# One fused two-layer kernel: sums moved to VectorE in the first layer, seven products for the last 96 columns, and another order of the last block, the start and the flag's load

## The chip, the core and the metric

The kernel runs on one core of one Trainium2 chip. The metric is device time in microseconds (us) of one launch. All times below are such times, taken from several runs or from one profiled execution; which of the two is said each time. A core has TensorE (PE, with its weight loads shown apart as PEld), VectorE (DVE), ScalarE (ACT), GpSimd (POOL) and SyncE (SP), which here issues all DMAs.

## The reference

`x` has 4 x 512 rows of 512 numbers; there are two gated layers with 1376 hidden columns each. Everything is 32-bit floating point.

```python
def attn(x, w_gate, w_up, w_down):
    s = silu(x @ w_gate.T)
    k = int(0.5 * 1376)
    _, idx = top_k(-abs(s), k)        # the half of smallest size in each row
    s = s with those set to 0
    return (s * (x @ w_up.T)) @ w_down.T

def ffn(x, W_gate, W_up, W_down):
    return (silu(x @ W_gate.T) * (x @ W_up.T)) @ W_down.T

x = x + layernorm(attn(layernorm(x), ...))
x = x + layernorm(ffn(layernorm(x), ...))
```

## The kernel before, in words

The 2048 rows are 16 tiles of 128. **First layer**: eight `Unit`s of two tiles. Each tile is loaded, normed (`layernorm`, L112), transposed by TensorE and copied to `xT` (`normed_T`, L339). `products` (L381) makes the gate as plain matmuls (L404, six groups a unit) and the up projection as a 2 x 2 block product with seven instead of eight block products (class `Seven`, L132: p1, p6, p5, then p7, p2, then p4, p3, each of 2 chunks). Its left factors are sums of quarters of `xT`: `Unit.sums` calls `stationary_sums` (L116) with GpSimd, four operations on 128 x 256 into the tile `S`. A 32-bit matmul is two instructions on TensorE. `search` (L435) finds each row's median size in six steps, in which ScalarE counts (L456) and VectorE takes the next guess (L461 to L481); `turns` (L554) transposes the masked hidden values, 128 at a time, and ScalarE copies them out (L582, L584).

**Down projections** of both layers are `downs` (L233): seven products too, for one or two pairs of tiles, as steps p1, p5, p6 for each pair, then p7, p2, p4, p3 for all pairs. Each step loads its weight (640 KB, tag `wd`, three buffers, L230) when it is first used. `rest` in it (L263) adds the last 96 hidden columns. `out_norm` (L321) norms the output tile (`moments`, L98: statistics, aggregate, add on VectorE, a power on GpSimd), adds the residual `xr` on GpSimd (L331) or, for the final tile, on VectorE (L328), and stores it (L332).

**Second layer**: four `Block`s of four tiles. `Block.pair` (L652) makes two chunks of 128 hidden columns of gate and up by seven products each, five times; `down_sums` (L690) makes their sums `D` on GpSimd. `Block.rest` (L674) makes the last 96 hidden columns of gate (`fg`) and up (`fu`) with plain matmuls of 512 columns (L681). Then the next block's tiles are normed and this block's `finish` (L706) runs its two pairs together; the last block runs them one after the other, `finish([0])` and `finish([1])`.

Whether the quick search found the exact median is counted in `flags`. The flag `badi` (L851) is loaded by all engines at the end (`values_load`, L875), and a general version of the layers is run behind a branch (L876) if it isn't zero, which it is here.

**What sets the order**: Everything in `tc.block(schedule_with_timeline_sim=True)` (L873) is put in order by a planner when the program is built. It simulates the engines and gives each engine, when it is free, the ready instruction that comes first in the program's order. So an instruction's place in the program is its rank, and a stall in the simulation is filled by a later ready instruction. On the chip each engine keeps that order and waits on semaphores. `fill` in `products` (L394) writes out by hand where other units' steps rank between the groups of matmuls. At the start the program ranks the load of tile 0, its norm, the load of tile 1, then the first layer's gate weight in three pieces (`CH`, L61) and the rest (L743 to L751). 18 transposes of the identity (L85) run before tile 0 is ready.

PSUM has tags `pa`, `px`, `py`, `pt` with two buffers each; in SBUF tags `S`, `w` (`sg` and the search's copy) have one.

Of the kernel before, what the change touches and what calls it, by code (L numbers as in the profile page):

```python
# [31 lines left out]
def sandwich_kernel(  # L32
# [65 lines left out]
    def moments(src, nm, kind, n=1):  # L98

        bufs = 1 if kind == "f" else 5  # L100
        st = small.tile([P, n, 6], F32, tag="st" + kind, name=f"st_{nm}", bufs=bufs)
        for i in range(n):
            nc.vector.bn_stats(st[:, i, :], src[:, ts(i, H // n)])
# [8 lines left out]
    def layernorm(dst, src, nm, kind):  # L112
        mv, rs = moments(src, nm, kind)
        nc.vector.tensor_scalar(dst, src, mv[:, 0:1], rs, ALU.subtract, ALU.mult)
# [17 lines left out]
    class Seven:  # L132


        def __init__(self, nm, left, right, c12, c21, c22):
            self.left, self.right = left, right
            self.c12, self.c21, self.c22 = c12, c21, c22
            n = c12.shape[-1]
            self.pa, self.px, self.py = [bank(k, f"{k}{nm}")[:, :n] for k in ("pa", "px", "py")]
# [93 lines left out]
    def downs(work, pairs, key, w_d, wr, res, dst, nm, final=False):  # L233
# [4 lines left out]

        st = []
# [11 lines left out]
        def product(k, which, i=None):  # L251
# [4 lines left out]
            for p in [st[i]] if first else st:  # L256
# [25 lines left out]
        def p7():  # L282
            product("p7", PX)
            for p in st:
                pz.append(bank("pt", f"pz{nm}_{p[0][0]}")[:, :H2])
                rest(pz[-1], p, 1, hi, True)

        def p2():
            product("p2", PA)
            for p, z in zip(st, pz):  # L290
                tiles, left, last, pa, px, py, ya, yb = p
                rest(pa, p, 0, lo)
                nc.vector.tensor_add(yb[:, hi], yb[:, lo], px)  # L293
                nc.vector.tensor_add(yb[:, hi], yb[:, hi], py)
                nc.vector.tensor_add(yb[:, hi], yb[:, hi], z)
                nc.scalar.copy(ya[:, lo], pa)

        def p4():
            product("p4", PX)
            for p in st:  # L300
# [5 lines left out]
        def p3():  # L306
            product("p3", PY)
            for p in st:
# [3 lines left out]
                out_norm(work, tiles[0], ya, res, dst, nm, final)  # L312
# [6 lines left out]
        return heads + [p7, p2, p4, p3]  # L319

    def out_norm(work, t, y, res, dst, nm, final=False):  # L321
# [3 lines left out]
        if final:  # L325
            mv, rs = moments(y, f"o{nm}_{t}", "f", 2)
            nc.vector.tensor_scalar(y, y, mv[:, 0:1], None, ALU.subtract)
# [20 lines left out]
    class Unit:  # L348
# [25 lines left out]
        def sums(self):  # L374
# [3 lines left out]
                nc.gpsimd, a[:, :2], a[:, 2:], b[:, :2], b[:, 2:], s[:, 0], s[:, 1], s[:, 2]  # L378
# [175 lines left out]
        def turns(self, other=False):  # L554
# [4 lines left out]
            def turn(k, g0):  # L559
# [22 lines left out]
                nc.scalar.copy(hT[:, g0 : g0 + nf, :], pt[:, :nf, :])  # L582
                if nf < n:
                    nc.scalar.copy(end, pt[: isz[-1], nf, :])  # L584
# [39 lines left out]
    class Block:  # L624
# [49 lines left out]
        def rest(self, wg, wu):  # L674
# [239 lines left out]
```

## Time and profile before

| | us |
|---|---|
| Median of 3 runs (886.12 to 889.33) | 888.31 |
| The profiled execution's own time | 887.46 |
| Its span, first to last instruction | 885.5 |
| TensorE busy | 862.3 |
| VectorE busy | 511.8 |
| ScalarE busy | 300.9 |
| GpSimd busy | 180.3 |

Mean granted TensorE clock: 0.993 of full speed. The profile gives each group of instructions its source line, engine, operation, output and inputs by the program's names, and shapes. A row of waits says which engine and instruction stood idle, for whom (the one that came last), for how long in total, how often, and the longest. Ends of matmuls are modelled, so their bars overlap; the distance between starts is the pace. A "q" behind an engine's name means its instruction queue. Times in the timeline count from the span's start. The first layer takes about the first 450 us, the second the rest.

### The profile page before, as it was taken

The numbers are of one execution on the slowest core, as the hardware profiler recorded it, in microseconds if no ns is written. First come the engines' busy times: TensorE is split into PE (matmuls) and PEld (weight loads), VectorE is DVE, ScalarE is ACT, GpSimd is POOL, SyncE is SP. The second block draws the span as 40 slices with busy tenths as digits, with TensorE's granted clock in tenths as the row PEclk, the third lists the DMA queues.
The fourth block names the chain that finished last, engine by engine and source line by source line (L and its number), as shares of the span: only waits on it lengthen the run. The fifth ranks groups of instructions, "written<-read, shape, count | busy, mean of one in ns | idle before, by whom it ended". The sixth has DMA issues, their size and how long they took to land. (4 is left out here: it accounts for less than half of the span.)

```text
span 885.5 us, 10211 instructions
## 1 busy us (share of the span) xinstructions
PE 862.3 (97%) x3588; PEld 652.4 (74%) x3588; DVE 511.8 (58%) x1328; ACT 300.9 (34%) x598; POOL 180.3 (20%) x249
## 2 busy tenths in 40 slices
PE   8999999999999899999999999999999999999995
PEld 5656566757667576677788888888788888888784
DVE  4887776775939578766955434554236443444322
ACT  2465575748463757466011111011101112011100
POOL 2120111212212112110433211321203221122221
PEclk9999999999999999999999999999999999999998
DMA  9999413334232343377374003610045002420064
GB/s 317 360 335 345 165 54 119 120 101 143 78 119 98 103 138 102 119 293 262 132 254 150 0 1 113 195 44 0 30 143 167 1 0 65 143 97 1 30 217 156
DMA packets 62924, 117.54 MB, mean 133 GB/s; under 512 B 4816, under 2 KB 36560, under 8 KB 62864
## 3 DMA queue, kind: packets, MB, share of 16 engines
q1 hardware_dynamic: 62864, 116.80, 39.4%
q8 instruction: 30, 0.49, 0.2%
q14 instruction: 30, 0.25, 0.1%
HBM read 97.91 MB, written 18.87 MB: 132 GB/s over the span
## 5 line engine op out<-in xcount | busy, mean ns | idle before, releaser
L456 ACT ACTIVATE ja<-v,cur 128x1376 bf16<-128x1376 f32 x96 | 138.3, 1441 | 76.9 <-DVE cur L481 54.4
L404 PE MATMUL pg<-wg,xT 128*128 128x456 f32 (+1 forms) x384 | 158.0, 559 | 3.4 <-ACT p L408 2.5
L404 PEld LDWEIGHTS pg<-wg,xT 128*128 128x128 f32 x384 | 73.2, 193 | 68.6 <-issue 59.9
L118 POOL TENSOR_TENSOR D<-hTb 128x256 f32<-128x256 f32 x20 | 14.6, 730 | 180.5 <-DVE hTb L672 180.5
L461 DVE TENSOR_SCALAR low<-cur 128x2 int32<-128x2 f32 x48 | 8.7, 181 | 72.0 <-ACT ja L456 72.0
L143 PE MATMUL pau<-wu,xT 128*128 128x344 f32 x128 | 43.6, 452 | 0.0
L143 PE MATMUL pagb<-xTb,wg 128*128 128x256 f32 x160 | 41.4, 379 | 0.0
L143 PE MATMUL paub<-xTb,wu 128*128 128x256 f32 x160 | 41.3, 380 | 0.0
L143 PE MATMUL pxub<-T,wu 128*128 128x256 f32 x160 | 41.2, 380 | 0.0
L143 PE MATMUL pxgb<-T,wg 128*128 128x256 f32 x160 | 41.1, 379 | 0.0
L258 PE MATMUL pad<-wd_p,hT 128*128 128x256 f32 x160 | 39.4, 380 | 1.3 <-DMA wd_p<-in_L_attn_w_down_dram 1.3
L408 ACT ACTIVATE p<-pg 128x456 f32<-128x456 f32 (+1 forms) x48 | 26.0, 544 | 43.1 <-PE pg L404 39.5
L258 PE MATMUL pxdb<-wdb_p,hTb 128*128 128x256 f32 x160 | 36.7, 379 | 2.1 <-DMA wdb_p<-sum_f 2.1
L258 PE MATMUL pxd<-wd_p,hT 128*128 128x256 f32 x160 | 37.2, 380 | 1.5 <-DVE y L293 1.5
L258 PE MATMUL padb<-wdb_p,hTb 128*128 128x256 f32 x160 | 37.1, 379 | 0.9 <-DMA wdb_p<-in_L_ffn_W_down_dram 0.9
L258 PE MATMUL pydb<-wdb_p,D 128*128 128x256 f32 x160 | 37.9, 379 | 0.1
L258 PEld LDWEIGHTS pxd<-wd_p,hT 128*128 128x128 f32 x160 | 30.3, 190 | 7.4 <-DVE y L293 1.7
L258 PEld LDWEIGHTS padb<-wdb_p,hTb 128*128 128x128 f32 x160 | 30.3, 190 | 7.2 <-issue 3.3
L258 PEld LDWEIGHTS pxdb<-wdb_p,hTb 128*128 128x128 f32 x160 | 30.3, 190 | 6.7 <-issue 2.5
L258 PEld LDWEIGHTS pad<-wd_p,hT 128*128 128x128 f32 x160 | 29.6, 190 | 7.4 <-DMA wd_p<-in_L_attn_w_down_dram 1.7
L258 PEld LDWEIGHTS pydb<-wdb_p,D 128*128 128x128 f32 x160 | 30.1, 190 | 6.2 <-issue 2.5
L670 ACT ACTIVATE sg<-sg 128x768 f32<-128x768 f32 x20 | 16.9, 843 | 50.9 <-DVE sg L167 50.9
(221 smaller groups left out, 1721.9 us busy)
## 6 DMA issues: line engine op xcount, KB each, us to landing
wd_p<-sum_a SPq DMA_DIRECT2D x28, 640.0 KB, 4.0
wd_p<-in_L_attn_w_down_dram SPq DMA_DIRECT2D x21, 640.0 KB, 4.2
wdb_p<-sum_f SPq DMA_DIRECT2D x20, 640.0 KB, 4.1
wdb_p<-in_L_ffn_W_down_dram SPq DMA_DIRECT2D x15, 640.0 KB, 4.2
xn<-in_x_dram SPq DMA_DIRECT2D x16, 256.0 KB, 3.1
xr<-in_x_dram SPq DMA_DIRECT2D x16, 256.0 KB, 2.8
x<-y SPq DMA_DIRECT2D x16, 256.0 KB, 2.0
xnb<-x SPq DMA_DIRECT2D x16, 256.0 KB, 3.1
```

The lines of the kernel that those rows point to most:

```text
L118: eng.tensor_add(s1, a21, a22)
L143: nc.tensor.matmul(ps, self.left[k][:, c, :], self.right[k][:, c, :], start=first and c == 0, stop=c == 1, skip_group_check=not first,)
L258: nc.tensor.matmul(p[which], p[1](k, c), ws[k][:, c, :], start=first and c == 0, stop=c == HC - 1, skip_group_check=not first,)
L404: nc.tensor.matmul(pg, self.xT[:, i, c, :], wg[:, c, c0:c1], start=(c == 0), stop=(c == NH - 1),)
L408: nc.scalar.activation(p[:, c0:c1], pg, AF.Silu)
L456: nc.scalar.activation(junk, v, AF.Sign, bias=cur[:, 0, i : i + 1], accum_out=cur[:, 1, i : i + 1],)
L461: nc.vector.tensor_scalar(low, cur[:, 1, :], 0.0, None, ALU.is_gt)
L670: nc.scalar.activation(sg[:, 1:, :], sg[:, 1:, :], AF.Silu)
```

## The change

1. `Unit.sums`: the four sums are made by VectorE instead of GpSimd.
2. `turns(True)` (only the last unit but one): the second tile's copies go from ScalarE to VectorE.
3. `downs`: the addition of `px` to `yb` moves from step p2 to p7; the remaining two additions become a step `c22`, called at the end of p2, or in the last block alone. In the last block both pairs run together, in the order p7, c22, p3, then p4 and p2 for the first pair and for the second. The last output's first half is read straight from PSUM by the statistics and the subtraction.
4. `Block.rest`: the last 96 columns of gate and up are one 2 x 2 block product (gate and up above each other, tiles left and right) by `Seven`. The sums of its weights are made once, by VectorE.
5. At the start the first piece of the gate weight is loaded before tile 1, and six transposes of the normed tile 0 into the unused `warm` are added.
6. `values_load` and the branch move into the planned stretch.

```diff
-    def moments(src, nm, kind, n=1):
+    def moments(parts, nm, kind):
+        n = len(parts)
...
-        for i in range(n):
-            nc.vector.bn_stats(st[:, i, :], src[:, ts(i, H // n)])
+        for i in reversed(range(n)):
+            nc.vector.bn_stats(st[:, i, :], parts[i])
...
-            n = c12.shape[-1]
-            self.pa, self.px, self.py = [bank(k, f"{k}{nm}")[:, :n] for k in ("pa", "px", "py")]
+            m, n = c12.shape
+            self.pa, self.px, self.py = [bank(k, f"{k}{nm}")[:m, :n] for k in ("pa", "px", "py")]
...
         def p7():
             product("p7", PX)
             for p in st:
+                tiles, left, last, pa, px, py, ya, yb = p
+                nc.vector.tensor_add(yb[:, hi], yb[:, lo], px)
                 pz.append(bank("pt", f"pz{nm}_{p[0][0]}")[:, :H2])
                 rest(pz[-1], p, 1, hi, True)
 
-        def p2():
-            product("p2", PA)
+        def c22():
             for p, z in zip(st, pz):
                 tiles, left, last, pa, px, py, ya, yb = p
-                rest(pa, p, 0, lo)
-                nc.vector.tensor_add(yb[:, hi], yb[:, lo], px)
                 nc.vector.tensor_add(yb[:, hi], yb[:, hi], py)
                 nc.vector.tensor_add(yb[:, hi], yb[:, hi], z)
-                nc.scalar.copy(ya[:, lo], pa)
...
+        def p2(part=slice(None)):
+            product("p2", PA, None, part)
+            for p in st[part]:
+                tiles, left, last, pa, px, py, ya, yb = p
+                rest(pa, p, 0, lo)
+                if not final:
+                    nc.scalar.copy(ya[:, lo], pa)
+            if not final:
+                c22()
+            else:
+                for p in st[part]:
+                    tiles, left, last, pa, px, py, ya, yb = p
+                    if p is st[-1]:
+                        out_norm(work, tiles[0], ya, res, dst, nm, pa)
+                    else:
+                        nc.scalar.copy(ya[:, lo], pa)
+                        out_norm(work, tiles[0], ya, res, dst, nm)
...
-                out_norm(work, tiles[0], ya, res, dst, nm, final)
+                if not final:
+                    out_norm(work, tiles[0], ya, res, dst, nm)
...
-        return heads + [p7, p2, p4, p3]
+        if not final:
+            return heads + [p7, p2, p4, p3]
+
+        ends = [lambda f=f, i=i: f(slice(i, i + 1)) for i in range(len(pairs)) for f in (p4, p2)]
+        return heads + [p7, c22, p3] + ends
...
-        if final:
-            mv, rs = moments(y, f"o{nm}_{t}", "f", 2)
-            nc.vector.tensor_scalar(y, y, mv[:, 0:1], None, ALU.subtract)
+        if pa is not None:
+            parts = [pa, y[:, H2:]]
+            mv, rs = moments(parts, f"o{nm}_{t}", "f")
+            for i in range(2):
+                nc.vector.tensor_scalar(
+                    y[:, ts(i, H2)], parts[i], mv[:, 0:1], None, ALU.subtract
+                )
             nc.vector.scalar_tensor_tensor(y, y, rs, xr, ALU.mult, ALU.add)
...
             self.left = stationary_sums(
-                nc.gpsimd, a[:, :2], a[:, 2:], b[:, :2], b[:, 2:], s[:, 0], s[:, 1], s[:, 2]
+                nc.vector, a[:, :2], a[:, 2:], b[:, :2], b[:, 2:], s[:, 0], s[:, 1], s[:, 2]
             )
...
-                nc.scalar.copy(hT[:, g0 : g0 + nf, :], pt[:, :nf, :])
+                copy = nc.vector.tensor_copy if other and k else nc.scalar.copy
+                copy(hT[:, g0 : g0 + nf, :], pt[:, :nf, :])
                 if nf < n:
-                    nc.scalar.copy(end, pt[: isz[-1], nf, :])
+                    copy(end, pt[: isz[-1], nf, :])
...
-        def rest(self, wg, wu):
+        def rest(self, left):
...
-            pg, pu = bank("pa", f"fg{nm}"), bank("px", f"fu{nm}")
-            for ps, w in ((pg, wg), (pu, wu)):
-                for c in range(NH):
-                    nc.tensor.matmul(
-                        ps[:n, :], w[:, c, 2 * HF :], self.xT[c // 2][:, c % 2, :],
-                        start=(c == 0), stop=(c == NH - 1),
-                    )
+            t = self.work.tile([P, 4, N2], F32, tag="w", name=f"sgr{nm}", bufs=1)[:n]
+            m = Seven(f"rb{nm}", left, self.right, t[:, 0, :], t[:, 1, :], t[:, 2, :])
+            m.first()
+            c11 = m.second()
             h = self.big.tile([P, N], F32, tag="b5", name=f"hTb{nm}_r")
-            nc.scalar.activation(h[:n, :], pg[:n, :], AF.Silu)
-            nc.vector.tensor_mul(h[:n, :], h[:n, :], pu[:n, :])
+            lo, hi = h[:n, :N2], h[:n, N2:]
+            nc.scalar.activation(lo, c11, AF.Silu)
+            m.third()
+            nc.scalar.activation(hi, m.c12, AF.Silu)
+            nc.vector.tensor_mul(lo, lo, m.c21)
+            nc.vector.tensor_mul(hi, hi, m.c22)
...
+            if not general:
+                for i in range(6):
+                    nc.tensor.transpose(warm[:, i % 4, :], units[0].x[0][:, :P], ident)
+            wg = load_weight(wpool, a_wg, "wg", f"1{nm}", CH[:1])
             units[0].load(1)
-            wg = load_weight(wpool, a_wg, "wg", f"1{nm}", CH)
+            load_weight(wpool, a_wg, wg, f"1{nm}", CH[1:])
...
+            t = work.tile([P, 3, 2, I - 2 * HF], F32, tag="S", name=f"wrs{nm}", bufs=1)
+            rest = stationary_sums(
+                nc.vector,
+                *[w[:, 2 * c : 2 * c + 2, 2 * HF :] for w in ws for c in range(2)],
+                t[:, 0], t[:, 1], t[:, 2],
+            )
...
-                block.rest(*ws)
-                if last:
-                    block.finish([0], wr)
-                    block.finish([1], wr, True)
-                else:
+                block.rest(rest)
+                if not last:
                     for k in range(TB):
                         blocks[b + 1].norm(k)
                     blocks[b + 1].sums()
-                    block.finish([0, 1], wr)
+                block.finish([0, 1], wr, last)
...
-    nbad = nc.values_load(badi[0:1, 0:1], min_val=0, max_val=2 * P * NTT)
-    with tc.If(nbad > 0):
-        layers("g", True)
+        nbad = nc.values_load(badi[0:1, 0:1], min_val=0, max_val=2 * P * NTT)
+        with tc.If(nbad > 0, label="general"):
+            layers("g", True)
```

More of the change, by code (lines that the diff above doesn't have):

```diff
@@ L112, in layernorm @@
     def layernorm(dst, src, nm, kind):
-        mv, rs = moments(src, nm, kind)
+        mv, rs = moments([src], nm, kind)
         nc.vector.tensor_scalar(dst, src, mv[:, 0:1], rs, ALU.subtract, ALU.mult)
@@ L249, in begin, with product @@
             st.append((tiles, left, last, pa, px, py, ya, yb))
-        def product(k, which, i=None):
+        def product(k, which, i=None, part=slice(None)):
             if k not in ws:
@@ L255, in product @@
             first = i is not None
-            for p in [st[i]] if first else st:
+            for p in [st[i]] if first else st[part]:
                 for c in range(HC):
@@ L284, in p7, with p4 @@
             for p in st:
+                tiles, left, last, pa, px, py, ya, yb = p
+                nc.vector.tensor_add(yb[:, hi], yb[:, lo], px)
                 pz.append(bank("pt", f"pz{nm}_{p[0][0]}")[:, :H2])
                 rest(pz[-1], p, 1, hi, True)
-        def p2():
-            product("p2", PA)
+        def c22():
             for p, z in zip(st, pz):
                 tiles, left, last, pa, px, py, ya, yb = p
-                rest(pa, p, 0, lo)
-                nc.vector.tensor_add(yb[:, hi], yb[:, lo], px)
                 nc.vector.tensor_add(yb[:, hi], yb[:, hi], py)
                 nc.vector.tensor_add(yb[:, hi], yb[:, hi], z)
-                nc.scalar.copy(ya[:, lo], pa)
-        def p4():
-            product("p4", PX)
-            for p in st:
+        def p2(part=slice(None)):
[15 more added lines that the diff above has]
+                        out_norm(work, tiles[0], ya, res, dst, nm)
+        def p4(part=slice(None)):
+            product("p4", PX, None, part)
+            for p in st[part]:
                 tiles, left, last, pa, px, py, ya, yb = p
@@ L304, in p4, with p3 @@
                 out_norm(work, tiles[1], yb, res, dst, nm)
-        def p3():
-            product("p3", PY)
-            for p in st:
+        def p3(part=slice(None)):
+            product("p3", PY, None, part)
+            for p in st[part]:
                 tiles, left, last, pa, px, py, ya, yb = p
@@ L318, in downs, with out_norm @@
         ]
-        return heads + [p7, p2, p4, p3]
-    def out_norm(work, t, y, res, dst, nm, final=False):
+        if not final:
+            return heads + [p7, p2, p4, p3]
+        ends = [lambda f=f, i=i: f(slice(i, i + 1)) for i in range(len(pairs)) for f in (p4, p2)]
+        return heads + [p7, c22, p3] + ends
+    def out_norm(work, t, y, res, dst, nm, pa=None):
         xr = work.tile([P, H], F32, tag="xr", name=f"xr{nm}_{t}")
         nc.sync.dma_start(xr, res[ts(t, P), :])
-        if final:
-            mv, rs = moments(y, f"o{nm}_{t}", "f", 2)
-            nc.vector.tensor_scalar(y, y, mv[:, 0:1], None, ALU.subtract)
+        if pa is not None:
[5 more added lines that the diff above has]
+                )
             nc.vector.scalar_tensor_tensor(y, y, rs, xr, ALU.mult, ALU.add)
```

## The prediction

> **What bounds the kernel now.** First the page's busy shares, then the waits of TensorE, because an engine at 97% leaves 23.2 us in all to be won by shuffling other work; then stretches of the start and the end.
>
> ```profile
> PE 862.3 (97%) x3588; PEld 652.4 (74%) x3588; DVE 511.8 (58%) x1328; ACT 300.9 (34%) x598; POOL 180.3 (20%) x249
> ```
> ```profile
> PE pg L404 <- ACT p L408: 2.5, 1, 2.5
> PE pxdb L258 <- DMA wdb_p<-sum_f: 2.1, 1, 2.1
> PE warm L86 <- POOL ident masks.py:199: 1.7, 1, 1.7
> PE pxd L258 <- DVE y L293: 1.5, 1, 1.5
> ...
> PE padb L258 <- DMA wdb_p<-in_L_ffn_W_down_dram: 0.9, 1, 0.9
> ```
> TensorE sets the time. Its waits are few and can be named, and they sum to 14.0 us; another 8.7 us lie after its last matmul (876.8 to 885.5). A wait costs about 0.16 more than its row, because a matmul's bar (0.38 for 256 columns) is longer than its pace (0.216: ten of them from 852.35 to 854.51). So the time changes only by matmul columns, by these waits, by the clock, and by the two ends. No row has TensorE waiting for S, the sums that move to VectorE.
>
> The start, by stretches of 3.4 us (columns: stretch, length, busy of PE, PEld, DVE, ACT, POOL with counts, PEclk, DMA share, GB/s), and one stretch near the end to compare:
>
> ```profile
> 5.30:8.70 3.40, 1.69 (x12) 1.03 (x10) 1.09 (x2) 1.29 (x4) 1.28 (x3) 1.00 1.03 388
> 8.70:12.10 3.40, 3.40 (x5) 1.66 (x6) 0.00 (x0) 0.00 (x0) 1.95 (x3) 0.50 1.04 400
> 12.10:15.50 3.40, 3.40 (x10) 1.57 (x10) 1.51 (x4) 1.24 (x3) 0.00 (x0) 0.99 1.05 372
> ...
> 862.00:865.40 3.40, 2.18 (x11) 1.57 (x9) 0.42 (x1) 0.00 (x0) 0.06 (x1) 1.00 0.93 273
> ```
> After a stretch in which TensorE was busy 1.69 of 3.40 us the clock is halved for the next: 5 gate matmuls where the following stretch has 10. After 2.18 of 3.40 it is not.
>
> The end, from the timeline and the instructions of the flag's load:
>
> ```profile
> 876.22 0.60 PE L264 MATMUL pydb<-wr,hTb_r 96*128 96x256 f32 x2
> 876.79 1.26 POOL L331 TENSOR_TENSOR yb<-yb,xrb 128x512 f32<-128x512 f32 x1 [0.66 <-DVE yb L114]
> 876.85 0.42 DVE L311 TENSOR_TENSOR yb<-yb,pydb 128x256 f32<-128x256 f32 x1
> ...
> 878.24 0.72 POOL L109 TENSOR_TENSOR rs_ob<-ve_ob,nhalf 128x1 f32<-128x1 f32 x1 [0.19 <-DVE ve_ob L107]
> 879.00 0.75 DVE L328 SCALAR_TENSOR_TENSOR yb<-yb,rs_ob,xrb 128x512 f32<-128x512 f32 x1 [0.44 <-POOL rs_ob L109]
> ```
> ```profile
> L875 SPq TENSOR_LOAD <-badi x1: 520/520/520, 880.2 to 880.2; - x1
> L875 SPq FUSED_REGOPS  x1: 186/186/186, 880.8 to 880.8; - x1
> ```
> After the last store is issued (879.8), SyncE loads the flag, checks it and branches at 881.1; its next instruction comes at 883.6.
>
> **Last 96 columns as seven products (certain).** Out: 16 matmul instructions of 512 columns a block, paced 0.429 (eight from 837.81 to 841.24), 6.86 us. In: 7 products x 2 chunks x 2 instructions = 28 of 256 columns, paced 0.216, 6.05 us. Four blocks: -3.3 us. The seven depend on one another through PSUM: p7 may not write px before ScalarE's copy (0.37) and VectorE's sum (0.42) have read it, and the copy's tile shares its only buffer with sg, which L672 frees at 839.5. In the last block the first three products would run 838.0 to 840.6, copy and sum 839.5 to 840.3: just in time. Bound: nothing, or 0.8 us a block (3.2 in all) if the cover is gone; I take 0.5. Behind a waiting p7 stand p2, p4, p3 and the down products, all of TensorE's queue, so such a wait counts in full. VectorE gets six operations of about 0.42 a block for one of 0.68, in a layer where it is busy 43%. The four sums of the weights (192 columns, once) lie under other matmuls. The work that used to lie under POOL's sums D of the fifth chunk (fu, 837.8 to 841.2) is replaced by 6.0 us of the same kind, so D (done 842.5) stays covered.
>
> **The last block's two pairs together.** Each weight is loaded once, not twice: 7 loads of 640 KB where there were 14. The waits of 0.9 and 2.1 go, with 0.16 each: 3.4 us (the stretches show DMA 0.93 to 1.06 busy there). What is late next: a weight is now used for 20 matmuls, 4.3 us, and its load takes 4.0 to 4.2 in the median, three buffers deep, so they just keep up. Ends 0 and -3.4; I take -3.4, since the earlier blocks run this way without any such row. The outputs' residual loads (256 KB) and stores go to SyncE's queue with p4 and p2; the last weight load stands before all stores, so no weight waits behind one.
>
> **The tail's norm.** The last operation reads PSUM directly, so add L311 (0.42 and a gap of 0.04) goes. But POOL's add for the tile before, L331, now starts later against the last matmul: that tile's chain from its last matmul (873.91) to L331's end (878.05) is 4.14, and only 12 matmuls (2.6) follow it, so POOL is free 1.55 after TensorE's end, where the power would be ready at 0.95. Power 0.55 and L328 0.75 then end at about 2.95, against 2.93 now (879.75 less 876.82). I take 0; ends -0.5 and +0.2. The split subtraction lies under the power.
>
> **The flag's load inside the planned stretch.** The flag is known at 448.5, so the planner can put the loads far ahead of the end. On SyncE 0.9 us (880.2 to 881.1) leave the path from the last store to the branch: -0.9, if the store has landed by then; packets of it run until 882.2, and the next instruction would come at 882.7. Elsewhere a load of 0.5 to 0.6 us falls mid-run on every queue; TensorE's ran at 874.1 beside matmuls without a gap. Ends -0.9 and +0.5.
>
> **The start.** The first weight piece passes tile 1 (256 KB, 0.7 us at 360 to 390 GB/s), so the first gate matmul moves from 8.63 to about 7.9: -0.7. Tile 1's four transposes (0.11 each) move behind it into paid time: +0.4. The six extra transposes (0.65) fill a gap. Now the clock. [...]gaps of 0.74 and 0.92 were enough. In the new stretch I count 0.3 of the first transposes, 0.4, 0.65, and 0.8 of gate matmuls, 2.2 busy of 3.4, like the stretch that kept its clock. Then the half-speed stretch (1.9 us lost, five spacings of 0.77 for 0.39) goes: -2.2 in all. Ends 0 (clock lost, work merely begun sooner) and -2.6; I take -2.2.
>
> **First layer.** Sums S: 32 operations leave POOL (29.1 us) for VectorE. There 256 columns cost 0.42, on the line through 344 columns (0.51) and 512 (0.69): 13.4 us, 1.7 for each of eight units, in stretches where VectorE is busy 68 to 81%. Since no wait ends in S, the move saves nothing itself. In return VectorE no longer stands behind POOL: L430 took 0.95 at 294.0 beside a POOL sum, otherwise 0.51. Queued behind the new operations are the search steps that ScalarE's counts wait for, and behind those the PSUM evictions. That chain caused the 2.5 wait (297.6), which also halved the clock for one stretch: 2.65 and 1.8. The added VectorE work costs between nothing and several such jams; I take +1.0, about the waits on D and c that stand there (0.8 and 0.2). The p7 addition placed earlier frees px: the wait "pxd <- DVE y L293" goes, -1.6 (ends 0, -1.6). Three copies of the second tile to VectorE relieve "ph <- ACT hT" (1.4) or do not: 0 taken.
>
> Sum: -3.3 + 0.5 - 3.4 - 0.9 - 2.2 + 1.0 - 1.6 = -9.9. The profiled execution, 887.5 (span 885.5 and 2.0 around it), becomes 877.6; it lies 0.9 under the median 888.3, so on the median **878.4**.
>
> **Rivals.**
> Jams dissolve: a new order of the queues also loses the 2.5 wait with its clock (4.4) and the 1.4: -9.9 - 4.4 - 1.4 = -15.7, 872.6. For it: these are accidents of order; against: VectorE has more to do.
> Only the firm parts: clock lost at the start (0), the L293 wait stays: -9.9 + 2.2 + 1.6 = -6.1, 882.2. For it: two rows, 1.69 and 2.18, bracket where the clock is lost[...].
> The seven products and the loads stall: the first cost 3.2 instead of 0.5 (+2.7), the 3.4 is not won (+3.4: a load of 4.2 against 4.3 of use leaves no room), and the start gives 0 (+2.2): -9.9 + 8.3 = -1.6, 886.7; the change would then not do what it says. For it: both margins are thin; against: the earlier blocks keep up with the same loads.
> VectorE as the bound of the first layer (slower): each jam costs 4.4 by the one seen (2.65 and 1.8). With 9.9 won elsewhere, it decides from the third new jam; slower by 0.5% takes 14.3, so four in eight units: 17.6 - 9.9 = +7.7, 896.0. For it: 81% in the stretch 30 to 85; against: there TensorE doesn't wait at all today.
>
> **How the numbers follow.** Forecast 0.50, jams dissolve 0.19, firm parts 0.18, stalls 0.07, VectorE bound 0.06. The bound of 0.5%, about what a measurement of this kernel can tell from no change, lies at 883.9 and 892.8. Faster: the first three less 0.03 for their upper edge, 0.84; same: 0.07 and that 0.03, 0.10; slower 0.06. The range, 871.0 to 884.0, takes in the first three cases; outside are the other two (0.13) and about 0.06 at the edges of the three.
>
> **What would show it.** Right: 112 matmuls of 256 columns for the last 96 with no row of waits; no DMA wait after the last block's first products; clock 1.00 between 8.7 and 12.1; SyncE's branch within 0.5 us of the last store's issue; no row for L293. Wrong: waits for c or the copies in that group, a DMA row of 1 us or more, 0.50 in the first stretches, or new ScalarE and VectorE rows before 450 that sum to over 5 us.

## The result, and the profile after

| | before | after |
|---|---|---|
| Median, 6 runs each on one chip | 887.16 (885.12 to 889.33) | 876.65 (875.72 to 881.22) |
| The profiled execution's own time | 887.46 | 876.47 |
| Its span | 885.5 | 874.5 |
| TensorE's last matmul ends at | 876.81 | 863.32 |
| VectorE's last operation ends after that by | 2.94 | 4.04 |
| and the span ends after that by | 5.79 | 7.10 |

The ratio is 0.9893, 95% interval 0.9874 to 0.9912: 9.5 us at 887.16 (the two medians lie 10.5 apart). The forecast was 878.4. The sum came out nearly right, but its terms did not: one term was too small by over 4 us, and two others cost time. The six executions of after lie 5.5 us apart, and each profile below shows one execution, so a difference of 1 to 3 us between two profiles need not come from the kernels.

The busy row of the page after. GpSimd lost 28.5 us and VectorE gained 10.6:

```profile
PE 854.4 (98%) x3642; PEld 659.2 (75%) x3642; DVE 522.4 (60%) x1393; ACT 302.0 (35%) x601; POOL 151.8 (17%) x217
```

TensorE's waits after (for whom, us in total, times, longest):

```profile
PE pad L260 <- DMA wd_p<-in_L_attn_w_down_dram: 2.6, 1, 2.6
PE pg L432 <- ACT p L436: 1.8, 2, 1.7
PE warm L86 <- POOL ident masks.py:199: 1.7, 1, 1.7
PE ph L606 <- ACT he L613: 1.0, 1, 1.0
PE pt L372 <- DVE xn L115: 0.9, 2, 0.6
PE pxgb L144 <- DVE sg L160: 0.3, 1, 0.3
...
```

The rows for `wdb` (2.1 and 0.9) and for `y` at L293 (1.5) are gone. The row of ScalarE's `p` shrank from 2.5 to 1.8 (its longest wait 1.7). The row of `wd_p` doubled, from 1.3 to 2.6; it is at 450.8, the first down projection after the first layer's search has ended.

The start, in the stretches shown of before:

```profile
5.30:8.70 3.40, 3.12 (x17) 2.06 (x16) 1.58 (x4) 0.65 (x2) 0.34 (x2) 1.00 1.05 406
8.70:12.10 3.40, 3.40 (x13) 1.81 (x12) 0.55 (x1) 1.47 (x5) 0.36 (x1) 1.00 1.05 390
12.10:15.50 3.40, 3.40 (x11) 1.67 (x10) 2.68 (x10) 1.43 (x5) 0.71 (x2) 1.00 1.06 370
```

TensorE is busy 3.12 of the first 3.40 us (before: 1.69), and the clock stays whole: 1.00 from 8.70 to 12.10, where before had 0.50.

The end, from the timeline, and SyncE's flag load, branch and next instructions:

```profile
862.72 0.60 PE L266 MATMUL padb<-wr,hTb_r 96*128 96x256 f32 x2
...
864.75 1.26 POOL L359 TENSOR_TENSOR yb<-yb,xrb 128x512 f32<-128x512 f32 x1 [1.68 <-DMA xrb<-x]
865.97 0.60 POOL L110 TENSOR_TENSOR rs_ob<-ve_ob,nhalf 128x1 f32<-128x1 f32 x1
...
866.61 0.75 DVE L356 SCALAR_TENSOR_TENSOR yb<-yb,rs_ob,xrb 128x512 f32<-128x512 f32 x1 [0.44 <-POOL rs_ob L110]
```
```profile
L913 SPq EVENT_SEMAPHORE  x8: 17/17/17, 870.9 to 871.5; - x8
...
L913 SPq COMPARE_BRANCH  x1: 45/45/45, 867.8 to 867.8; - x1
```
```profile
L912 SPq TENSOR_LOAD <-badi x1: 669/669/669, 443.7 to 443.7; - x1
```

SyncE's last ten waits, after, and then before:

```profile
L947 SPq EVENT_SEMAPHORE  x10: 17/28/28, 871.6 to 874.4; - x10
```
```profile
L910 SPq EVENT_SEMAPHORE  x10: 17/28/28, 884.2 to 885.5; - x10
```

GpSimd's addition for the tile before the last stands 1.68 waiting for a residual, so the last power begins 2.65 after TensorE's end (863.32), where the prediction had it ready at 0.95 with GpSimd free at 1.55. SyncE's flag load did move to 443.7, and the branch comes 0.39 after the last store is issued (867.39). But the next instruction comes 3.1 after the branch, before it came 2.5 after. And the last ten waits take 2.8 for 1.3, because SyncE stands still for 1.6 after the first of them (871.57 to 873.18). So the end changed by -0.9 at the branch, +0.6 right behind it and +1.6 at this second stop.

**Where the 11.0 us of the profiled execution went.** For this I went through TensorE's matmuls in the two traces. Each has a pace by its width (128 columns 0.109, 256 0.216, 344 0.289, 456 0.383, 464 0.389, 512 0.429, the medians of the distances between starts). What a distance exceeds this by is time lost; it holds waits and halved clock alike.

| Term | forecast | measured | how |
|---|---|---|---|
| Seven products | -3.3 | -3.3 | 4 x (16 x 0.429 - 28 x 0.216) |
| New waits in the second layer | +0.5 | +0.6 | lost 480 to 800: -0.15, now 0.42 |
| Last block | -3.4 | -3.9 | lost from 800 on: 3.85, now -0.02 |
| Start | -2.2 | -1.9 | lost 0 to 50: 3.99, now 1.47; six transposes +0.65 |
| First layer | -0.6 | -5.0 | lost 50 to 480: 13.92, now 8.88 |
| Norm at the tail | 0 | +1.1 | 2.94, now 4.04 |
| Flag and what follows | -0.9 | +1.3 | 5.79, now 7.10 |
| Sum | -9.9 | -11.1 | own times: 887.46 - 876.47 = 11.0 |

The row of the first layer has two parts: 50 to 400 us lost 7.4, now 4.0, and 400 to 480 lost 6.5, now 4.8.

### The profile page after: what moved, and what is told of

The parts are those of the page before. It is cut to its first block, busy times and chain, and to the rows that moved or that the text cites. A ratio compares the mean times of both kernels' runs of the same rounds, so it can differ in the third digit from the quotient of the medians.

```text
span 874.5 us, 10346 instructions
## 1 busy us (share of the span) xinstructions
PE 854.4 (98%) x3642; PEld 659.2 (75%) x3642; DVE 522.4 (60%) x1393; ACT 302.0 (35%) x601; POOL 151.8 (17%) x217
## 4 chain that ended last, share of the span: by engine, by line
PE 64%; DVE 14%; DMA 8%; issue 5%; ACT 5%; SPq 2%; POOL 1%; ACTq 0%; POOLq 0%; DVEq 0%
PE pg L432 7%; PE pxgb L144 6%; PE pxub L144 6%; PE pxdb L260 4%; ACT ja L484 4%; PE pxd L260 4%; PE pyub L144 4%; PE pagb L144 4%; PE pygb L144 4%; PE paub L144 4%; PE padb L260 3%; PE pydb L260 3%; PE pyd L260 3%; PE pxu L144 2%; PE pad L260 2%
## 5 line engine op out<-in xcount | busy, mean ns | idle before, releaser
L432 PE MATMUL pg<-wg,xT 128*128 128x456 f32 (+1 forms) x384 | 155.1, 549 | 1.8 <-ACT p L436 1.8
L144 PEld LDWEIGHTS pxgb<-T,wg 128*128 128x128 f32 x160 | 30.2, 190 | 4.6 <-DVE sg L160 0.6
L144 PEld LDWEIGHTS pxub<-T,wu 128*128 128x128 f32 x160 | 30.2, 190 | 4.5 <-DVE hTb L160 0.3
```

The costliest lines, as they stand in the source:

```text
L144: nc.tensor.matmul(ps, self.left[k][:, c, :], self.right[k][:, c, :], start=first and c == 0, stop=c == 1, skip_group_check=not first,)
L432: nc.tensor.matmul(pg, self.xT[:, i, c, :], wg[:, c, c0:c1], start=(c == 0), stop=(c == NH - 1),)
```

## The experiments

Theory A: GpSimd's sums S held VectorE up in the first layer, and moving them freed it. Rival B: the first layer gained only because another order of the queues came out. Further questions were the start's worth, the residual at the tail, and the flag.

A view used throughout: "unit 2 to unit 8" is the time from the first gate matmul of the second unit to that of the eighth. It leaves out the start and everything after about 348 us. Before it took 305.0 (42.2 to 347.2), after 300.9 (40.3 to 341.2).

### S back on GpSimd, the rest of the change kept

```diff
-                nc.vector, a[:, :2], a[:, 2:], b[:, :2], b[:, 2:], s[:, 0], s[:, 1], s[:, 2]
+                nc.gpsimd, a[:, :2], a[:, 2:], b[:, :2], b[:, 2:], s[:, 0], s[:, 1], s[:, 2]
```

> The changed kernel with one part undone: the sums S of the first layer are made by GpSimd again. 'Lost time' is what TensorE's matmul starts fall behind their median pace between 50 us and the flag's cast: 12.1 us before the change, 6.2 after it (the wait at 37 us counted). Theory A ([...]GpSimd's 29 us of S held VectorE up): VectorE's other first-layer operations get 8 to 10 us longer in sum, lost time goes back to 10 to 13, the median to 881 to 883. Rival B (only the planner's new order moved the jams): VectorE's operations may lengthen, but the lost time stays at 5 to 8 and the median at 876 to 878.

Measured: 887.08 (882.88 to 889.24), ratio to before 1.0003 (0.9985 to 1.0021). The whole gain is gone, though the rest of the change was left in. Lost time between 50 and 480 us is 20.5 (after: 8.9), unit 2 to unit 8 takes 308.0. VectorE's operations other than S, in the first 480 us and counted where both kernels have the same number, take 13.2 us longer than after; before to after they got 10.1 us shorter. An example of VectorE's groups, before and then after (behind the bar stand busy us and mean ns of one):

```profile
L463 DVE COPY_PREDICATED lo<-low,cur 128x4 f32<-128x4 int32 x48 | 10.9, 226 | 1.0
```
```profile
L491 DVE COPY_PREDICATED lo<-low,cur 128x4 f32<-128x4 int32 x48 | 7.8, 162 | 1.0
```

The operations are the same, and the mean hides what happened: in before five of the 48 took 0.60 to 1.12 us and the others at most 0.17, after none took more than 0.17. Four of the five ran beside a sum of S. Two larger cases, from the timeline of before:

```profile
292.32 0.69 DVE L470 TENSOR_TENSOR d<-cur,lo 128x4 f32<-128x4 f32 x1
...
293.87 0.73 POOL L121 TENSOR_TENSOR S<-xT,S 128x256 f32<-128x256 f32 x1
294.02 0.95 DVE L430 TENSOR_TENSOR p<-p,c 128x344 f32<-128x344 f32 x1
```

This can be counted in all traces. For each VectorE operation of the first 480 us take what it lasts beyond the short end (tenth percentile) of the same operation in all fourteen traces, and put that down to the GpSimd operation that it overlaps longest. Beside the 32 sums of S this gives 8.9 us in before, nearly all in 20 operations, and 8.5 to 9.4 in each of the other four kernels that make S on GpSimd. Beside GpSimd's other work it is 12.1 in before and 10.7 after. So the 10 us are mostly meetings with S, in both orders of the queues that these five kernels have, and the first half of theory A is shown: S lengthens VectorE's work. The second half is what of that reaches TensorE.

TensorE's waits in this run, with S on GpSimd again, end in VectorE and ScalarE and none in S:

```profile
PE pg L432 <- ACT p L436: 3.0, 2, 1.5
PE pad L260 <- DMA wd_p<-in_L_attn_w_down_dram: 2.0, 1, 2.0
PE pxu L144 <- DVE c L154: 1.8, 1, 1.8
PE pz L266 <- DVE badi L885: 1.7, 1, 1.7
...
PE pxu L144 <- DVE low L489: 1.2, 1, 1.2
PE pau L144 <- ACT c L153: 1.0, 1, 1.0
```

One of them (1.8) can be followed in the timeline:

```profile
218.42 1.88 POOL L110 TENSOR_TENSOR rs_o<-ve_o,nhalf 128x1 f32<-128x1 f32 x1 [9.79 <-DVE ve_o L108]
...
220.34 0.55 DVE L115 TENSOR_SCALAR y<-y,mv_o,rs_o 128x512 f32<-128x512 f32 x1 [0.44 <-POOL rs_o L110]
...
220.97 1.27 POOL L359 TENSOR_TENSOR y<-y,xr 128x512 f32<-128x512 f32 x1 [0.67 <-DVE y L115]
221.13 1.13 DVE L489 TENSOR_SCALAR low<-cur 128x2 int32<-128x2 f32 x1
...
226.82 1.43 PE L144 MATMUL pxu<-wu,xT 128*128 128x344 f32 x4 [1.84 <-DVE c L154]
```

The power takes 1.88 (after: 0.55) beside a VectorE operation of 1.64, then VectorE's compare of two elements takes 1.13 (after: 0.16) beside GpSimd's addition, and TensorE then waits 1.84. VectorE stood idle for 0.44 of the power's delay and lost 0.97 in the compare; that the whole wait comes from there isn't shown. So in this jam each engine's work took longer beside the other's. But the partner in this jam is an addition that both kernels have, not S. So not every jam here is one with S. Nor does all the lost time come from S: 8.4 of the 20.5 us lie between 400 and 480 us, where the run with the flag outside (below) loses 8.1 with S on VectorE.

### Before, with S alone on VectorE

The edit is the reverse, in the kernel before.

> The kernel before with one part alone: the sums S by VectorE. Theory A: VectorE's other first-layer operations get 8 to 10 us shorter in sum, the lost time falls from 12.1 to 5 to 8, the median to 881 to 884. Rival B: the jams move but stay 9 to 13 in sum, 886 to 890. The slower rival of the prediction (VectorE as the bound) would show lost time over 20 and a median over 890.

Measured: 884.55 (882.08 to 886.61), ratio 0.9978 (0.9967 to 0.9989): only some 2 us. Yet unit 2 to unit 8 takes 295.9, 9.1 less than before, and only 1.5 are lost between 50 and 400 (before: 7.4). VectorE's other operations became 5.1 us shorter, where theory A had said 8 to 10: the meetings with S are gone, but those with GpSimd's other work grew by 3.7 (by the count above). The rest of the kernel took the gain back. From 0 to 50 us 6.0 are lost for 4.0, as the halved clock at the start lasted twice as long; from 400 to 480 us 8.4 for 6.5, by two rows of its waits above all (the second again with a halved clock behind it; the mean granted clock of this execution is 0.991, of before 0.993):

```profile
PE pad L258 <- DMA wd_p<-in_L_attn_w_down_dram: 2.2, 2, 1.3
PE ph L578 <- ACT he L584: 2.1, 1, 2.1
```

### GpSimd kept busy for nobody: sums that read, and memsets that don't

Two kernels put extra work on GpSimd beside the kernel after, whose S stays on VectorE. Nothing of the computation changes.

```diff
             self.sums()
+            if not self.nm.startswith("g"):
+                dm = work.tile([P, 2, 96], F32, tag="dm", name=f"dm{nm}_{j}", bufs=1)
+                for _ in range(5):
+                    nc.gpsimd.tensor_add(dm, wg[:, 0:2, :96], wg[:, 2:4, :96])
```
```diff
             self.sums()
+            if not self.nm.startswith("g"):
+                dm = work.tile([P, 192], F32, tag="dm", name=f"dm{nm}_{j}", bufs=1)
+                for _ in range(11):
+                    nc.gpsimd.memset(dm, 0.0)
```

> The kernel after, unchanged in its results, with five additional GpSimd sums of 192 columns in each of the first layer's eight units, at the place where the sums S are made. They read two tiles of the gate weight, write a scratch tile, and nobody waits for them; S stays on VectorE. Theory A [...]: VectorE's other first-layer operations get 7 to 13 us longer in all, as in the run with S on GpSimd; the eighth unit begins 346 us or later (after: 341.2), and the time is 881 to 889. Rival B (S on GpSimd costs because TensorE gets S late, or because of the order of the queues alone): nobody waits for these sums, so VectorE's operations keep their length within 3 us, the eighth unit begins at 339 to 345, and the time stays 874 to 880.

> As the run with the additional GpSimd sums, but with eleven memsets of 192 columns in their place: GpSimd is kept about as long (some 2.9 us a unit by the line through its memsets of 2 and 128 columns, 98 and 204 ns), stands in the same place of its queue, but reads nothing. Theory A in its narrow form [...]: VectorE's operations with two inputs keep their length[...]; less than half of the loss of the other run, 875 to 881. Rival: what costs is GpSimd's queue being occupied, so that the powers of the norms behind it come late: then this run loses as much as the other one with sums, and the norms' powers show longer waits.

Measured: with the sums 885.8 (884.89 to 892.6), ratio 0.9996 (0.9979 to 1.0014); with the memsets 876.94 (875.03 to 879.11), ratio 0.9893 (0.9863 to 0.9923). The times are those of theory A, but the traces say less. As nobody holds the extra work back, all forty sums (and 88 memsets) ran in the first 44 us, not spread over the units. The kernel with memsets keeps the order of after in every queue; the one with sums does not, from 10 us on, so the two differ in more than the reading. In the first 44 us VectorE's groups read, with the sums, with the memsets, and in the kernel after:

```profile
L127 DVE TENSOR_TENSOR wus<-wu 128x688 f32<-128x688 f32 x2 | 2.5, 1260 | 0.0
L129 DVE TENSOR_TENSOR wu<-wu 128x688 f32<-128x688 f32 x2 | 2.5, 1258 | 0.0
```
```profile
L127 DVE TENSOR_TENSOR wus<-wu 128x688 f32<-128x688 f32 x2 | 1.7, 870 | 0.9 <-DMA wu<-in_L_attn_w_up_dram 0.9
L129 DVE TENSOR_TENSOR wu<-wu 128x688 f32<-128x688 f32 x2 | 1.7, 867 | 0.0
```
```profile
L127 DVE TENSOR_TENSOR wus<-wu 128x688 f32<-128x688 f32 x2 | 1.8, 876 | 1.5 <-DMA wu<-in_L_attn_w_up_dram 1.5
...
L129 DVE TENSOR_TENSOR wu<-wu 128x688 f32<-128x688 f32 x2 | 1.7, 868 | 0.0
```

What this shows firmly: beside GpSimd's sums an unchanged VectorE sum takes 1258 ns for 868, beside memsets 867; GpSimd's own sums took 818 ns in the mean, 586 at their shortest. Over the first layer VectorE's same operations took 6.9 us longer with the sums (theory A: 7 to 13), 0.5 shorter with the memsets; by the count above 5.8 lie beside the sums and 0.2 beside the memsets. These are means: beside GpSimd's sums the VectorE sum took 1.45 times as long (1258 for 868). In before no meeting with S cost a VectorE operation more than 0.83, and a sum of S lasts 0.72 at the shortest. By what way the two hold each other up is not shown.

What it does not show: that 7 us on VectorE are 11 on TensorE. Lost time of this run lies in one place, 11.5 us before 50 us. There TensorE waited 2.8 for a VectorE that was busy without a pause, its sums lengthened: theory A. Then sixteen sums in a row (27.0 to 43.3) stood before a norm's power in GpSimd's queue, VectorE idled 3.9 for that power, TensorE waited 4.9, and the clock was halved for 10 us (granted 0.50 from 42.0 to 49.0, and 0.77 in the 3.5 us on either side): that is the other rival, an occupied queue. From 50 to 400 us, where the sums are over, 4.7 are lost against 4.0.

### What S on GpSimd is worth between unit 2 and unit 8

All kernels of this study (us from unit 2 to unit 8). Kernels of one row have the same order of instructions in all five queues up to unit 8, compared one by one (the extra memsets left out):

| Same order | S by | us |
|---|---|---|
| before; before, new rest; before, new downs | GpSimd | 305.0, 302.7, 306.9 |
| before, new start; after, S on GpSimd | GpSimd | 305.6, 308.0 |
| after; flag outside; early residual; with memsets | VectorE | 300.9, 301.0, 304.3, 302.4 |
| after, no extra transposes; combined, first and second | VectorE | 299.0, 299.2, 299.8 |
| before, S on VectorE | VectorE | 295.9 |
| with sums | VectorE | 302.2 |

The means are 305.6 with S on GpSimd and 300.5 with S on VectorE: 5.1 us. Within one row, where the order can't be the reason, single executions lie up to 4.2 apart, and the row means of one maker differ by 1.9 (GpSimd) and up to 6.3 (VectorE). No two kernels here differ in S and not also in the order. So the 5 us hold VectorE's shorter operations, the new order and some chance of the execution, and how they divide is not shown. Theory A is right that S lengthens VectorE's work; rival B, that the order alone did it, is neither shown nor shut out for what reaches TensorE.

### The six extra transposes taken out

```diff
-            if not general:
-                for i in range(6):
-                    nc.tensor.transpose(warm[:, i % 4, :], units[0].x[0][:, :P], ident)
```

> The changed kernel without the six extra transposes at the start. If a gap of a fraction of the 3.4 us stretch is enough to halve the clock (the rows of before): TensorE is busy about 2.2 to 2.5 of 3.4 in the stretch from 5.3, near the line between 1.69 and 2.18; with the clock lost 1.5 to 2 us more, 878 to 879; with the clock kept no change, 876 to 877. [...]

Measured: 872.92 (872.16 to 874.46), ratio 0.9847 (0.9826 to 0.9868): faster than after, which neither forecast had (876 to 877, or 878 to 879). The gate matmuls come 0.77 apart until 11.2, half the pace (0.389), and unit 2 begins at 41.8, 1.5 later than after. In this execution the pace was not lost but not yet whole: the transposes before come 0.213 apart too, where the whole pace is 0.109 (the profile's granted clock reads 1.00 from 5.3 on). So the run doesn't tell whether the gap would have halved the clock. But the wait for ScalarE's `p` at 292 fell from 1.66 to 0.2, and unit 8 begins at 340.8, 0.4 earlier than after; the weight wait at 450 is 1.3 for 2.6. A head start of 1.5 us at the beginning was given back in full.

### Before, with the new start alone

The transposes and the order of the loads (point 5 of the change) in the kernel before.

> The kernel before with the change's start alone: six transposes on tile 0 and the first piece of the gate weight ahead of the other pieces. Theory A (a head start is given back inside the first layer as long as GpSimd's sums hold VectorE up): the first gate matmul moves from 8.6 to about 7.2, the clock is kept, the second unit begins about 1.9 earlier, but the eighth still begins at 346 to 348, and the time is 885.5 to 888. The prediction's step (2.2 us at the start come off the end): 884 to 885, the eighth unit at 345.

Measured: 892.72 (890.82 to 894.28), ratio 1.0073 (1.0049 to 1.0097): slower by 6 us, which neither had expected. The start itself does what it should: first gate matmul at 7.4 (before: 8.6), no halved clock before 50 us, where 0.85 are lost for 3.99, unit 2 at 39.7 for 42.2. Of these 2.5, 1.9 are still there at unit 8 (345.3), so my sentence that the first layer swallows them was wrong here. Then comes a wait that before does not have, of 2.9, and the three matmuls from 415.49 behind it take 1.14, where their whole pace is 0.38 + 2 x 0.216 = 0.81:

```profile
PE pg L404 <- ACT p L408: 2.9, 2, 1.5
PE pxd L258 <- DMA wd_p<-sum_a: 2.9, 1, 2.9
PE pad L258 <- DMA wd_p<-in_L_attn_w_down_dram: 2.5, 2, 1.4
```

SyncE's queue around it, from the timeline:

```profile
400.06 0.52 SPq L832 DMA_DIRECT2D wus<-sum_u  x1
401.65 0.52 SPq L832 DMA_DIRECT2D wu<-sum_u  x1
402.21 2.02 SPq L834 DMA_DIRECT2D wu<-in_L_ffn_W_up_dram  x3
404.59 0.92 SPq L840 DMA_DIRECT2D wu<-in_L_ffn_W_up_dram  x1
405.60 0.67 SPq L230 DMA_DIRECT2D wd_p<-sum_a  x1
```

The first layer's down weight is issued behind 3.4 MB of the second layer's weights and used at 415.5, 9.9 later; such a load took 4.6 in the median in the stretch 385 to 450 of before. Yet before has these loads in the same order:

```profile
404.25 1.65 SPq L836 DMA_DIRECT2D wu<-in_L_ffn_W_up_dram  x1
406.00 0.99 SPq L230 DMA_DIRECT2D wd_p<-sum_a  x1
```

What differs is TensorE's queue: there 40 matmuls on `D` and 12 transposes into `ptb` stand before the weight's use at 418.3, here 20 and 4 before 415.5. So the new start gave TensorE another order, and this order wants the weight before it has come. The kernel after with S put back has the same SyncE order here and no such wait, but it too has all 40 before the use. Lost time of 400 to 480 is 10.2 for 6.5.

### The new last 96 columns and the new down projections, each alone

Points 4 and 3 of the change, each in the kernel before.

> The kernel before with one part alone: the last 96 columns as seven products. By the count of columns -3.3 us and at most +0.5 for new waits in the second layer: 883 to 884 against before's 886 to 887. Rival (the seven wait for one another): new rows of waits for c or the copies of 0.5 us or more a block, 885 to 887. The first layer keeps S on GpSimd, so by theory A its lost time between 50 and 400 us stays at 6 to 13 us (7.6 before, 12.2 with S put back, 1.6 to 4.4 in the runs with S on VectorE).

> The kernel before with one part alone: the down projections' new order (px added in p7, both pairs of the last block together, the last output's half from PSUM). The prediction's terms: the two DMA waits of the last block go (-3.4), the wait on L293 goes (-1.6), the tail 0: 882 to 883. What the changed kernel's trace adds: the tail costs +1.1 (the late residual): 883 to 884. By theory A the first layer's lost time between 50 and 400 us stays at 6 to 13 us.

Measured: the seven products 884.53, ratio 0.9963 (0.9951 to 0.9976), so -3.3 at the 886.96 of before measured with it (interval -2.1 to -4.3): as worked out. The down projections 885.37 (882.15 to 887.73), ratio 0.9982 (0.9969 to 0.9995): -1.6, where 3 to 4 had been expected. In its trace the last block's loss does go (3.85 to 0.15), but VectorE ends 4.85 after TensorE for 2.94, and the span 7.24 after that for 5.79: 3.4 given back at the tail. And the wait for `y` (1.5 in before) is 1.4 there: VectorE's queue has the same order as in before up to 854.6 us, so ranking the addition earlier moved it nowhere in the first layer. Lost time between 50 and 400 us is 5.0 and 9.1, for 7.4 of before with the same order; the first is below the 6 to 13 that theory A had said.

### The tail: the residual loaded earlier, and the flag at the end

```diff
-        xr = work.tile([P, H], F32, tag="xr", name=f"xr{nm}_{t}")
+        late = dst is out and t - NTT in (-1, -3)
+        kw = dict(tag="xn", bufs=3) if late else dict(tag="xr")
+        xr = work.tile([P, H], F32, name=f"xr{nm}_{t}", **kw)
```

> The changed kernel, with the residual of the last block's second pair loaded into other buffers, so that the load need not wait for the first pair's outputs. After the change VectorE ended 4.0 us behind TensorE (2.9 before), and GpSimd's last addition waited 1.7 us for that load. Theory E (the load is what is late): that wait goes, VectorE ends 2.9 to 3.1 us behind TensorE, the median is 1 us lower, 875.5. Rival F (GpSimd's order is: its addition stands before the last power anyway): 3.8 to 4.1 as now, 876.6.

Measured: 878.1 (876.77 to 880.44), ratio 0.9895 (0.9872 to 0.9918), no gain. The tail did what was looked for: VectorE ends 3.03 after TensorE (after: 4.04), and no wait for `xrb` stands before the last power:

```profile
864.80 0.60 PE L266 MATMUL padb<-wr,hTb_r 96*128 96x256 f32 x2
...
867.04 0.60 POOL L110 TENSOR_TENSOR rs_ob<-ve_ob,nhalf 128x1 f32<-128x1 f32 x1
...
867.67 0.75 DVE L358 SCALAR_TENSOR_TENSOR yb<-yb,rs_ob,xrb 128x512 f32<-128x512 f32 x1 [0.44 <-POOL rs_ob L110]
```

So the 1.1 of the tail is the residual's: two `xr` buffers for four outputs that now follow closely, and a load that waits for a store. The first layer did not change: TensorE, VectorE, ScalarE and GpSimd have the order of after to the end, SyncE up to 672 us. Yet in this execution the wait for `p` (1.8 lost at 292.8 in after) is 2.2 at 294.5, with a halved clock behind it (the mean granted clock is 0.994, of after 0.995), and a wait of 1.4 at 73 is new. So the order of these queues is not what made the median higher. Then the flag:

```diff
-        nbad = nc.values_load(badi[0:1, 0:1], min_val=0, max_val=2 * P * NTT)
-        with tc.If(nbad > 0, label="general"):
-            layers("g", True)
+    nbad = nc.values_load(badi[0:1, 0:1], min_val=0, max_val=2 * P * NTT)
+    with tc.If(nbad > 0):
+        layers("g", True)
```

> The changed kernel with the flag's load and the branch put behind the planned stretch again. From the last operation on VectorE to the end took 5.8 us before and 7.1 after the change. Theory C (the new place costs[...]): 5.8 again, the median 1.3 lower, about 875.3. Rival D (the place saves SyncE's 0.9 as predicted, and the 7.1 has another cause): the load returns to the end, 8.0, the median about 877.5.

Measured: 878.73 (876.06 to 880.24), ratio 0.9906 (0.9878 to 0.9933); the interval holds the ratio of after, so nothing is shown in the time. The span ends 7.63 after VectorE, with the flag inside 7.10. The flag's load does cost 0.9 there: the branch comes 1.30 after the last store's issue and not 0.39. But the next instruction comes 2.7 after the branch and not 3.1, which leaves 0.5. The +1.3 has its cause elsewhere. It comes with the new down projections: all ten kernels with them take 6.9 to 7.6 from VectorE's end and have the second stop among SyncE's last waits, 1.3 to 2.0 long; the four without them take 5.8 to 6.0 and stand nowhere longer than 0.43. In the run with the down projections alone it lies between 882.28 and 883.71. Packets of 8 KB of the instruction queue move in these microseconds, but in before they do so too (8 packets, 0.07 MB, from 875 on), so they don't tell what the stop is. Its cause is open.

### The combinations

First: after without the extra transposes, with the early residual, and with the flag's sum made in the second block. Second: the same, but the flag left where it is in after.

> The changed kernel without the six transposes, with the early residual load, and with the flag computed in the second block of the second layer (so that SyncE's load of it no longer stands before a weight load that TensorE waits for at 450 us). Theory: 872.9 of the run without the six, -1.0 for the tail, -0.5 to -1.0 for the weight wait: 871 to 872. Rival (what is saved at the flag turns into a longer wait for the same weight): 872 to 873.

> The kernel after without the six additional transposes at the start, and with the residual of the last two tiles' norms loaded into other buffers, so that it is loaded ahead. If the gains are independent: without the transposes alone 872.9, and the earlier residual gives 1.0 at the end (VectorE ends 3.0 after TensorE, not 4.0), so 871.9. If the load mainly shifts the order of the queues (as in the run with that alone, 878.1), 872 to 877.

Measured: 874.62 (873.23 to 877.3), ratio 0.9857 (0.9833 to 0.9881), and 872.7 (872.39 to 874.83), ratio 0.9847 (0.9822 to 0.9873). The later flag brought new waits in the second layer (lost 480 to 800: 1.8), and the weight wait at 450 that it was to shorten is 1.8, for 1.4 in the second; with the flag outside it was 1.9. So the flag's load is not what sets that wait. The second keeps every queue of TensorE, VectorE, ScalarE and GpSimd in the order of the kernel without transposes, and its tail is 3.02. Its ratio equals that kernel's, so the 1.15 of the tail can't be told from nothing in the medians. The intervals of these two (the second combination and the kernel without transposes) lie below that of after, if narrowly; that of the first combination does not.

## Why the prediction came out, point by point

**Seven products, right.** 3.3 in the ledger, and 3.3 by the run with that alone. The feared wait of p7 for the copy and the sum stayed small: 0.3 for `sg` once in four blocks.

**Last block, right.** The two load rows went, and no later load was late, although use (4.3) and load (4.0 to 4.2) were close.

**Tail's norm, wrong by 1.1.** The failed step is "POOL is free 1.55 after TensorE's end". I followed GpSimd's chain from its last matmul through norm and power, and left out that the addition has another input, the residual. Its load was named in the same prediction, as one that goes to SyncE's queue with p4 and p2, but only asked whether it delays weights, not whether it is late itself. The run with other buffers shows both.

**Flag, wrong in sign: -0.9 became +1.3.** The branch did come 0.9 earlier, 0.39 after the last store's issue. The step that failed is "the next instruction would come at 882.7", that is 2.5 after the branch as before, with the rest of the end unchanged. It came 3.1 after, and 1.6 more went at the second stop, which the prediction did not have. That stop belongs to the kernels with the new down projections, not to the flag; why is open.

**Start, right in its rows, not in its worth.** The clock was kept and the first matmul moved from 8.6 to 7.2. But executions of before alone range from 0.990 to 0.998 in mean clock, and one stretch of 3.41 us at half clock makes 0.002 of that (an estimate: half of 3.41 in 885), so the two halved stretches of the profile of before (from 8.7 and from 298.9) can't both be in all of them. Whether 2.2 us arrive at the end was taken for granted. Without the transposes the kernel is faster; with the new start alone it is slower than before. An earlier start is also another order.

On the clock itself the prediction went by two rows, 1.69 and 2.18 busy. The runs bear it out at the start: with 1.69 busy of 3.40 in gaps below 1 us the clock was halved (0.50), with 3.12 it was not (1.00), and all seven kernels with the transposes kept it in these first stretches. It is not wholly the transposes' doing: of seven kernels without them three kept it as well (the new down projections alone and both combinations), two lost it (before, and before with S on VectorE, 1.73 busy), and two were not yet at the whole pace (no extra transposes, 0.213 for 0.109, and the new rest alone). Nor is the busy share between 1.69 and 2.18 the rule: a stretch with 1.57 busy (new start alone, from 221.40) and one with 1.59 (unused sums, from 460.20) were followed by the whole clock. What decides stays open.

**First layer, mis-sized: -0.6 forecast, -5.0 measured.** This is the term that carried the result, while tail and flag took 3.3 more than forecast. The sentence that failed is "Since no wait ends in S, the move saves nothing itself." It looked for the gain where TensorE waits for GpSimd, and charged the sums to VectorE as added work. What the traces show in its place: 32 sums cost VectorE 13.3 us, and its other operations of the first 480 us became 10.1 us shorter, so the move was nearly free for VectorE and took 29 us from GpSimd. The prediction had one instance in hand (an operation of 0.95 beside a GpSimd sum, otherwise 0.51) and did not count how many there are: 20. How much of the 5.0 is due to this is not shown; 3.4 of it lie between 50 and 400 us, where S is made.

The other part of this term, -1.6 for the wait at L293, came true in its row and not by its mechanism. That row stays (1.4) with the new down projections alone, and it is gone with S alone on VectorE or with the new start alone, which don't touch the addition. It went with another order of the queues, by luck.

The rival "jams dissolve" (872.6) described the direction of this term better than the forecast: the 2.5 wait became 1.7 without a halved clock (1.00 from 293.4 to 303.6; before had 0.50 from 298.9 to 302.3). That the total met the forecast is partly luck: 4.4 more from the first layer, 3.3 less at the end.

**What stays open.** How the 5 us between unit 2 and unit 8 divide into VectorE's shorter operations, another order and chance. The run with unused sums could have told, had they been spread over the units; they ran early. Second, why the new down projections bring a stop of 1.3 to 2.0 us among SyncE's last waits.

## What to carry to other kernels

When work moves off GpSimd, look at the durations of VectorE's small operations, not only at who waits for GpSimd: a row whose mean lies well above its shortest case pointed here to meetings that would go (226 ns in the mean, 43 of the 48 at most 170). Whether TensorE gains from that is a second question. Here the parts of the change did not add: S alone gave 2.0, the rest of it without S nothing, together 9.5. Judge a part by a stretch that it can reach (unit 2 to unit 8), compare the order of the queues before calling a difference one of order (executions with the same order lay up to 4.2 us apart in that stretch), and try the whole with single parts taken out. And follow every input of the last chain, its DMA too, before calling a tail unchanged.

## What the runs showed of the hardware that I had not expected

GpSimd and VectorE operations that met took longer even where they have one or two elements a row: with S back on GpSimd a compare of VectorE took 1.13 for 0.16, a power of GpSimd 1.88 for 0.55. In before, 20 VectorE operations beside S lost 8.9 us. Memsets of GpSimd, 23.4 us in the first 32, lengthened next to nothing (0.2 us over 29 operations beside them; a sum took 867 for 868 ns). The halved clock (0.50) came after a short run of gaps, 1.69 us busy of 3.40, and once did not come at 1.57. And SyncE's first instruction after the branch around the general version came 2.5 to 3.2 us later, with a second stop of 1.3 to 2.0 in ten of the fourteen kernels.
